# A Swin layer with a dynamic convolution behind it: where the convolution's pieces and its taps stand in the order of the work

## The chip, the cores and the metric

The kernel runs on one core of a Trainium2 chip. The metric is the device time of one execution in microseconds. Before the change it was 3257.63 us, the median of 3 runs (3256.80 to 3258.41).

## What is computed

The input is x, 16 images of 192 channels and 56 x 56 pixels, in float32. Two layers follow one another:

```python
# layer 0: one Swin block, windows of 7 x 7, shifted by 3, 6 heads of 32
h = layernorm(x over channels); h = roll(h, -3, -3); cut into 64 windows of 49 tokens
q, k, v = h @ qkv_w + qkv_b
attn = softmax(q * 32**-0.5 @ k.T + rel_bias + mask) @ v
x1 = x + roll_back(attn @ proj_w + proj_b)
y = gelu(layernorm(x1) @ fc1_w + fc1_b) @ fc2_w + fc2_b      # 192 -> 768 -> 192
x = x1 + y
# layer 1: a depthwise 3 x 3 convolution whose taps depend on the image
pooled = x.mean over pixels
t = relu(gamma * (pooled @ w1.T - running_mean) / sqrt(running_var + eps) + beta)
taps = (t @ w2.T + b2) * causal_mask          # 4 of the 9 taps are not zero
out = depthwise_conv(x, taps) + bias
```

The taps of an image need the mean over all its pixels, so its convolution can start only when the image has left layer 0.

## The kernel before

**Steps.** An image is held in SBUF as two tiles: x0 for channels 0 to 127 and x1 for the other 64, upper half of the rows in partitions 0 to 63 and lower half in 64 to 127. Each has one more row 0 in front, which the convolution reads as the row above. A step `i` is one row of windows in each half of an image (16 windows, handled as eight by two); an image has STEPS = 4 steps, the whole input NS = 64. The main loop (L975) is a pipeline: its turn `i` does the MLP of step i-2 (mlp_first, mlp_wide, mlp_narrow), the attention of step i, q, k and v of step i+1, the layer-norm statistics of steps i+2 and i-1, and pieces of the convolution of the last finished image.

**Order.** The schedule is written out by hand (`tc.manual_schedule`): each engine runs its instructions in the order in which the program issues them; semaphores between engines are put in from the tiles. PSUM is four pairs of banks, `pair0` to `pair3`, taken by name through `banks(name, k)`; the four letters A, B_, C, D of a turn say which is which, and the turn ends with `pairs = [C, B_, D, A]`. So the next turn's first ph tile takes this turn's C, its second B_, its third D, its fourth A.

**One turn on TensorE**: ph (first MLP layer: three long and three short products, then f = 3 to 5 short; st, the statistics, in pair C; f = 3 to 5 long), sc (scores, first of them in pair C again), pq, pe, pk (q and k), pf (second MLP layer, wide half) with the transposes pt between, po (attention times v), pf (narrow half), pp (projection) and pv (v of the next step).

**What the change touches.**
- `attention_v_out` (L437) copies v from PSUM (two tiles pv, in pairs D and A; each has two banks, index h) to the block-diagonal operand `vbd` (L204): 16 copies, of which VectorE has those with j = 0 (L450) and ScalarE those with j = 1 (L452), two and two by turns.
- `norm1_scale` (L310) is twelve products into the window tiles (L328, L336), in the main loop on VectorE.
- `conv_begin` (L679) starts a piece of 14 rows on ScalarE (`y = tap1 * x + bias`, L683); `conv_rest` (L692) adds three taps on VectorE (L698), for pieces 3 and 5 with a copy of the bias into one row (L707), and issues the output DMAs on SP (L716, L718). An image has six pieces; `conv_ready(k)` hands out up to k.
- In a turn the first piece is in `between` (L986): behind three gelus and the three short products, ahead of the statistics and of `norm_vars` (L280 on ScalarE, L282 on VectorE). The second has its `conv_begin` at L1041, behind the gelu table load, and its `conv_rest` at L1050, between mlp_narrow and the narrow `mlp_out` (L641).
- `residual` (L571) adds the projection to x1 (L578, from pp1) and to x0 (L582, from pp).
- `taps_pool` and `taps` (L646 to L677) run once per image, in the turn in which its last step leaves the MLP: a sum (L648), three copies into the rows 0 (L650 on GpSimd, L651 and L652 on VectorE), four matmuls into a tile t of pair C, and five VectorE operations (L661 to L676) that end with the taps `wt`. They are issued behind v's matmuls and ahead of `attention_v_out` (L1064).
- `norm_squares` (L238) for the second norm: squares on ScalarE (L243, L244), a sum on GpSimd (L250).

Of the kernel before, what the change touches and what calls it, by code (L numbers as in the profile page):

```python
# [36 lines left out]
def tile_swin_then_dynamic_conv(  # L37
# [163 lines left out]


    kbd = one.tile([128, 3, NWIN, 2, N], F32, tag="kbd", name="kbd")
    vbd = const.tile([128, 2, NWIN, HEADS // 2, 64], F32, tag="vbd", name="vbd")  # L204
    prob = [
        const.tile([128, 2 * HEADS, 64], F32, tag=f"prob{i}", name=f"prob{i}") for i in range(4)
    ]
# [229 lines left out]
    def attention_v_out(pvs):  # L437

        for blk, pv in enumerate(pvs):
            src = pv.rearrange("p h (w n) -> p h w n", w=2)[:, :, :, 0:DIM]  # L440
            src = src.rearrange("p h w (g j d) -> p h w g j d", j=2, d=HD)
            for s in range(2):
                for j in range(2):
                    for h in range(2):
                        dst = vbd[j * 64 : j * 64 + N, h].rearrange(
                            "p (b w s) g (j d) -> p b w s g j d", b=2, s=2, j=2
                        )[:, blk, :, s, :, j, :]
                        f = src[s * 64 : s * 64 + N, h, :, :, j, :]
                        if j == 0:
                            nc.vector.tensor_copy(dst, f)  # L450
                        else:
                            nc.scalar.copy(dst, f)  # L452

    def attention_scores(i, q4, q2, ks):

# [62 lines left out]
    def attention_weigh(po, po1, wp, prt):  # L518
        for s in range(2):
            w = wp * 2 + s  # L520
            for a, g in ((0, 0), (0, 1), (1, 0), (1, 1), (0, 2), (1, 2)):

                r, k = (g, a) if g < 2 else (a, 2)
                o = po[:, a] if g < 2 else po1
                at = (g if g < 2 else a) * 64
                mm(
                    o[at : at + 64, w * N : (w + 1) * N],
                    vbd[:, a, w, g, :],
                    prt[:, r, k * PW + s * 64 : k * PW + s * 64 + N],
                    True,  # L530
                    True,
                )
# [17 lines left out]

    def project(i, o, k, k1):

        pp, pp1 = banks(f"pp_{i}", k), banks(f"pp1_{i}", k1)[:, 0]

        def narrow():
            for a in range(2):
                mm(pp1[a * 64 : a * 64 + 64, :T], wp0[:, C0:DIM], o[:, a], True, False)

        def rest():
            for a in range(2):  # L560
                p = slice(a * 64, a * 64 + 64)
                mm(pp[:, a, :T], wp1[p], o[p, 2], True, False)

        def whole():
            mm(pp1[:, :T], wp2, o[:, 2], False, True)
            for a in range(2):
                mm(pp[:, a, :T], wp0[:, 0:C0], o[:, a], False, True)

        return pp, pp1, narrow, rest, whole

    def residual(i, pp, pp1):  # L571
        v0, v1 = rows_of(i)
        q1 = pp1[:, :T].rearrange("p (r c) -> p r c", c=IMG)
        q0 = pp[:, :, :T].rearrange("p h (r c) -> p h r c", c=IMG)
        rolls = ((0, IMG - SHIFT, SHIFT), (IMG - SHIFT, IMG, 0))
        for lo, hi, to in rolls:
            xs = v1[:, :, to : to + hi - lo]
            nc.vector.scalar_tensor_tensor(xs, q1[:, :, lo:hi], pb[1], xs, ALU.add, ALU.add)  # L578
        for a in range(2):
            for lo, hi, to in rolls:  # L580
                xs = v0[:, a, :, to : to + hi - lo]
                nc.vector.scalar_tensor_tensor(xs, q0[:, a, :, lo:hi], pb[0], xs, ALU.add, ALU.add)  # L582

    def mlp_first(i, yn, hid, ks, between):
# [12 lines left out]

        for f in range(3):
            take(f)
            long(dsts[f], wf1, cols(f), y0, True)  # L600
        for f in range(3):
            short(dsts[f], wf1, cols(f), y1, False)
            gelu(f)
        for f in range(3, NFC):
            take(f)
            short(dsts[f], wf1, cols(f), y1, True)
        between()
        for f in range(3, NFC):
            long(dsts[f], wf1, cols(f), y0, False)
            gelu(f)  # L610
# [35 lines left out]
    def taps_pool(b):  # L646
        pooled = small.tile([128, 2, 1], F32, tag="pooled", name=f"pooled_{b}")
        nc.vector.tensor_reduce(pooled, sums.pop(b), AX.X, ALU.add)  # L648
        x0, x1 = images[b]
        nc.gpsimd.tensor_copy(x0[:, 0, :], x0[:, IMG, :])  # L650
        nc.vector.tensor_copy(x1[0:64, 0, :], x1[64:128, HALF, :])  # L651
        nc.vector.tensor_copy(x1[64:128, 0, :], x1[0:64, HALF, :])  # L652
        return pooled

    def taps(b, pooled, k):

        pt = banks(f"t_{b}", k)[:, 0]
        for kc in range(2):
            mm(pt[:, 0:RED], pooled[:, kc].broadcast_to([128, 128]), w1t[:, kc], kc == 0, kc == 1)
        tt = small.tile([128, 1, RED], F32, tag="tt", name=f"tt_{b}", bufs=1)  # L660
        nc.vector.tensor_tensor(tt[:, 0], pt[:, 0:RED], bn[:, 0], ALU.mult)  # L661
        nc.vector.tensor_tensor(tt[:, 0], tt[:, 0], bn[:, 1], ALU.add)
        tw = small.tile([128, 2 * NTAP, RED], F32, tag="tw", name=f"tw_{b}", bufs=1)
        nc.vector.scalar_tensor_tensor(
            tw,
            tt.broadcast_to([128, 2 * NTAP, RED]),
            0.0,
            w2n.rearrange("p k t r -> p (k t) r"),
            ALU.max,
            ALU.mult,  # L670
        )
        wt = small.tile([128, 2, NTAP], F32, tag="wt", name=f"wt_{b}")
        nc.vector.tensor_reduce(
            wt.rearrange("p k (t o) -> p (k t) o", o=1), tw, AX.X, ALU.add
        )
        nc.vector.tensor_tensor(wt, wt, b2t, ALU.add)  # L676
        return wt  # L677
# [72 lines left out]
    def tail_of(i, o, kp, kv):  # L750

        pvs, v_rest, v_whole = attention_v(i + 1, kv) if has(i + 1) else (None, None, None)
        if o is not None:
            pp, pp1, narrow, rest, whole = project(i, o, kp, 3)
# [83 lines left out]
    for t in [kbd, vbd] + prob:  # L838
        nc.gpsimd.memset(t, 0.0)
    keys = stats_of(-1)  # L840
    dev = norm_devs(keys)
# [66 lines left out]
    def taps_weights():  # L908
# [66 lines left out]
    for i in range(2, NS + 2):  # L975
        A, B_, C, D = pairs
        keys = {}


        if has(i + 1):  # L980
            norm1_scale(i + 1, dvs.pop(0), nc.vector)
        if (i + 3) % STEPS == 0 and (i + 3) // STEPS < B:
            b = (i + 3) // STEPS
            images[b] = load_x(b, nc.sync)

        def between():  # L986
# [9 lines left out]
        mlp_first(i - 2, yns.pop(i - 2), hid, (A, B_, C, D, A, B_), between)  # L996
        for part, dev in var:
            table(AF.Sqrt)
            norm_root(part)
# [46 lines left out]
        if has(i):  # L1046
            o = attention_rows(i, attention_values(i, prts, D, C))
        pf1 = mlp_narrow(i - 2, hid, A)
        for c in ys:
            conv_rest(*c)  # L1050
        mlp_out(i - 2, 1, pf1[:, :T])
        if has(i):
            pp, pp1, p_narrow, p_rest, p_whole = project(i, o, B_, C)
            p_narrow()
            p_rest()
        if has(i + 1):
# [1 line left out]
            v_rest()  # L1058
        if has(i):
            p_whole()  # L1060
            residual(i, pp, pp1)
# [87 lines left out]
```

## Time and profile before

| | |
|---|---|
| median of 3 runs | 3257.63 us |
| the profiled execution, its own time | 3261.49 us |
| its span, first to last instruction | 3259.7 us |
| granted TensorE clock, mean | 0.981 |
| busy: PE / DVE / ACT / POOL | 3128.8 / 2155.5 / 1855.1 / 1020.4 us |
| y taps L698 (VectorE), x288 | 321.0 us, mean 1116 ns |
| v's copies L450 (VectorE), x512 | 159.2 us, mean 349 ns |
| v's copies L452 (ScalarE), x512 | 135.4 us, mean 312 ns |

PE is TensorE's matmuls, PEld its weight loads, DVE is VectorE, ACT is ScalarE, POOL is GpSimd, SP issues the DMAs. A matmul in float32 stands as two instructions. In a timeline line the columns are: start and length in us, engine, line, operation, out<-in, shapes, how many; in brackets the idle time of the engine just before and what ended it. In the list of waits they are: who waited for whom, us in total, how often, the longest.

### The profile page before, as it was taken

Reading aid. Unit: us, or ns where it says so; the run is one execution under the profiler, and the core shown is the slowest. Engines: PE = TensorE matmul, PEld = TensorE weight load, DVE = VectorE, ACT = ScalarE, POOL = GpSimd, SP = SyncE. Lnnn points to the kernel's source line nnn. Section 1 sums busy time; section 2 is a strip of 40 time slices with the busy share of each in tenths; the row PEclk is TensorE's granted clock in tenths of the full one; section 3 lists DMA queues with packets and bytes.
Section 4 is the critical chain, followed back from the end, with each engine's and each line's share of the span. In section 5 each row is a group of like instructions: output and inputs, shape, how many; then the busy total and the mean of one; then the engine's idle time right before and its main releaser. Section 6 shows DMA issues by size and latency. Waiting matters only on the chain.

```text
span 3259.7 us, 64143 instructions
## 1 busy us (share of the span) xinstructions
PE 3128.8 (96%) x26130; PEld 1938.8 (59%) x26130; DVE 2155.5 (66%) x3893; ACT 1855.1 (57%) x2988; POOL 1020.4 (31%) x912
## 2 busy tenths in 40 slices
PE   5699999999999999999999999999999999999996
PEld 3456566666666656666666656666665666666653
DVE  4345666766767676676776766676676767667664
ACT  2445655655655665565665565565565565566552
POOL 4333233233233223333323323323323323323220
PEclk7699999999999999999999999999999999999998
DMA  3001012121111202102111111202111120201101
GB/s 99 12 19 48 20 40 56 31 60 31 33 53 36 61 26 65 31 26 60 37 51 36 54 29 39 55 30 62 31 32 55 36 59 28 65 25 31 26 31 45
DMA packets 79123, 135.35 MB, mean 42 GB/s; under 512 B 21766, under 2 KB 61692, under 8 KB 76908
## 3 DMA queue, kind: packets, MB, share of 16 engines
q1 hardware_dynamic: 77266, 128.54, 14.0%
q8 instruction: 206, 3.38, 0.4%
q0 software_dynamic: 1056, 1.92, 0.3%
q10 hardware_dynamic: 506, 0.79, 0.1%
q14 instruction: 89, 0.73, 0.1%
HBM read 41.25 MB, written 38.54 MB: 24 GB/s over the span
## 4 chain that ended last, share of the span: by engine, by line
PE 89%; DVE 4%; ACT 2%; issue 1%; POOL 0%; DMA 0%; ACTq 0%; DVEq 0%; POOLq 0%
PE ph L92 23%; PE pf L92 22%; PE pv L92 7%; PE pp L92 7%; PE po L92 5%; PE pq L92 4%; PE pt L509 4%; PE sc L92 4%; PE st L92 4%; PE pe L92 4%; PE pk L92 4%; DVE y L698 1%; DVE vbd L450 1%; DVE y L707 1%; ACT vbd L452 1%
## 5 line engine op out<-in xcount | busy, mean ns | idle before, releaser
L92 PE MATMUL ph<-yn,wf 128*128 128x392 f32 (+1 forms) x3072 | 811.4, 501 | 27.3 <-ACT vbd L452 18.8
L92 PE MATMUL pf<-hid,wf 128*128 128x392 f32 (+1 forms) x3072 | 802.8, 494 | 3.5 <-ACT hid L596 2.0
L496 POOL TENSOR_TENSOR prob<-e,tot 113x588 f32<-113x588 f32 x256 | 298.1, 1176 | 1165.8 <-DVE tot L495 1151.3
L92 PEld LDWEIGHTS ph<-yn,wf 128*128 128x128 f32 (+1 forms) x3072 | 425.4, 189 | 384.4 <-issue 91.6
L452 ACT COPY vbd<-pv 49x192 f32<-49x192 f32 x512 | 135.4, 312 | 768.1 <-DVE vbd L450 767.8
L92 PEld LDWEIGHTS pf<-hid,wf 128*128 128x128 f32 (+1 forms) x3072 | 386.4, 164 | 303.6 <-issue 119.9
L698 DVE SCALAR_TENSOR_TENSOR y<-x,wt,y 128x770 f32<-128x770 f32 x288 | 321.0, 1116 | 214.8 <-ACT y L683 208.1
L596 ACT ACTIVATE hid<-ph,f1b 128x784 f32<-128x784 f32 x384 | 336.8, 912 | 127.7 <-PE ph L92 127.3
L250 POOL TENSOR_TENSOR sq<-sq,sq 64x392 f32<-64x392 f32 x256 | 262.9, 1027 | 383.1 <-ACT sq L244 368.6
L347 POOL TENSOR_TENSOR yn<-x,dv 128x784 f32<-128x784 f32 x64 | 129.2, 2019 | 574.6 <-DMA dv<-dev 541.8
L92 PEld LDWEIGHTS pv<-wqkv,win 64*128 64x128 f32 (+1 forms) x2048 | 259.4, 190 | 47.5 <-DVE x L641 7.7
L92 PE MATMUL pv<-wqkv,win 64*128 64x192 f32 (+1 forms) x2048 | 277.1, 328 | 7.7 <-DVE x L641 4.4
L480 DVE TENSOR_TENSOR e<-sc,bias_t 113x588 f32<-113x588 f32 x256 | 179.6, 763 | 149.5 <-PE sc L92 149.4
L487 DVE TENSOR_TENSOR e<-e,top 113x588 f32<-113x588 f32 x256 | 265.7, 1038 | 8.9
L641 DVE SCALAR_TENSOR_TENSOR x<-pf,cols,x 128x784 f32<-128x784 f32 (+1 forms) x128 | 105.8, 827 | 232.8 <-PE pf L92 225.7
L92 PE MATMUL pp<-o,wp 128*128 128x392 f32 (+2 forms) x896 | 253.0, 517 | 2.6 <-ACT o L545 2.6
L235 ACT ACT_TABLE_LOAD x192 | 246.3, 1283 | 3.4
L515 ACT COPY prt<-pt 128x678 f32<-128x678 f32 x256 | 179.1, 726 | 118.1 <-PE pt L509 116.5
L490 ACT ACTIVATE e<-e 113x588 f32<-113x588 f32 x256 | 176.7, 691 | 107.6 <-DVE e L487 105.2
L450 DVE COPY vbd<-pv 49x192 f32<-49x192 f32 x512 | 159.2, 349 | 97.0 <-ACT vbd L452 82.9
L509 PEld LDWEIGHTS pt<-ident,prob 113*128 113x128 f32 x1536 | 167.3, 142 | 76.1 <-issue 47.0
L92 PE MATMUL po<-prt,vbd 128*64 128x49 f32 x6144 | 199.9, 225 | 0.2 <-ACT prt L515 0.2
(143 smaller groups left out, 4073.3 us busy)
## 6 DMA issues: line engine op xcount, KB each, us to landing
dv<-dev SPq DMA_DIRECT2D x1020, 49.0 KB
x<-in_x_dram SPq DMA_DIRECT2D x15, 1484.0 KB
out_dram<-y SPq DMA_DIRECT2D x48, 392.0 KB
out_dram<-y SPq DMA_DIRECT2D x48, 196.0 KB
x<-in_x_dram SPq DMA_DIRECT2D x16, 392.0 KB
x<-in_x_dram SPq DMA_DIRECT2D x15, 350.0 KB
out_dram<-y SPq DMA_DIRECT2D x16, 308.0 KB
out_dram<-y SPq DMA_DIRECT2D x16, 154.0 KB
```

Of the source, the lines that this page charges most:

```text
L92: nc.tensor.matmul(dst, lhs, rhs, start=start, stop=stop, skip_group_check=True)
L235: nc.scalar.activation(junk, eps_t[0:1], func)
L250: nc.gpsimd.tensor_tensor(s0[p, h], s0[p, h], s1[p], ALU.add)
L450: nc.vector.tensor_copy(dst, f)
L480: nc.vector.tensor_tensor(e, sc[:PW, :, : HEADS * N], rel, ALU.add)
L487: nc.vector.tensor_tensor(ehs[wp], ehs[wp], t.broadcast_to([PW, 2 * HEADS, N]), ALU.subtract)
L490: nc.scalar.activation(es[wp], es[wp], AF.Exp)
L496: nc.gpsimd.tensor_tensor(prob[wp][:PW, :, 0:N], ehs[wp], t.broadcast_to([PW, 2 * HEADS, N]), ALU.mult)
L509: nc.tensor.transpose(pt[:, a, g * PW : (g + 1) * PW], prob[wp][:PW, h : h + 2, :].rearrange("p h k -> p (h k)"), ident[:PW, :PW],)
L515: nc.scalar.copy(prt, pt[:, :, : 3 * PW])
L596: nc.scalar.activation(hid[:, f], phs[f][:, :, :T], AF.Gelu, bias=f1b[:, f : f + 1])
L698: nc.vector.scalar_tensor_tensor(dst, src, wt[:, kc, t : t + 1], dst, ALU.mult, ALU.add)
```

## The change

1. Conv: `conv_ready(2)` at the head of the turn. The first piece's `conv_begin` is issued at once, ahead of norm1_scale and of all gelus; a new `after()`, called in `mlp_first` behind the first three gelus, issues the second piece's `conv_begin` and then both `conv_rest`. The places in `between` and around `mlp_narrow` are gone.
2. v: `vbd` becomes two tiles, one per h. VectorE makes all copies of h = 0, ScalarE all of h = 1.
3. Taps: the sum and the four t matmuls are issued behind the projection's last matmuls, ahead of the residual and of v's long matmuls; t lies in the second bank of the pair whose first bank is pp1. In the residual, between its x1 and x0 parts, one add makes tt (`taps_hidden`). The copies into the rows 0, all three now on VectorE (`taps_rows`), and the rest of the network (`taps_out`) are issued behind `attention_v_out` and `norm_squares`. The multiplication of t by the batch norm's scale is gone; w1t is scaled once at the start instead, by two products.

```diff
-    vbd = const.tile([128, 2, NWIN, HEADS // 2, 64], F32, tag="vbd", name="vbd")
+    vbd = [
+        const.tile([128, NWIN, HEADS // 2, 64], F32, tag=f"vbd{h}", name=f"vbd{h}")
+        for h in range(2)
+    ]
...
-            for s in range(2):
-                for j in range(2):
-                    for h in range(2):
...
-                        if j == 0:
-                            nc.vector.tensor_copy(dst, f)
-                        else:
-                            nc.scalar.copy(dst, f)
+            for h, copy in enumerate((nc.vector.tensor_copy, nc.scalar.copy)):
+                for s in range(2):
+                    for j in range(2):
...
+                        copy(dst, src[s * 64 : s * 64 + N, h, :, :, j, :])
...
-    def residual(i, pp, pp1):
+    def residual(i, pp, pair1, between=None):
...
             nc.vector.scalar_tensor_tensor(xs, q1[:, :, lo:hi], pb[1], xs, ALU.add, ALU.add)
+        if between:
+            between()
         for a in range(2):
...
             short(dsts[f], wf1, cols(f), y1, False)
             gelu(f)
+        after()
...
+    def taps_rows(b):
+
         x0, x1 = images[b]
-        nc.gpsimd.tensor_copy(x0[:, 0, :], x0[:, IMG, :])
+        nc.vector.tensor_copy(x0[:, 0, :], x0[:, IMG, :])
         nc.vector.tensor_copy(x1[0:64, 0, :], x1[64:128, HALF, :])
         nc.vector.tensor_copy(x1[64:128, 0, :], x1[0:64, HALF, :])
...
+    def taps_hidden(b, pt):
         tt = small.tile([128, 1, RED], F32, tag="tt", name=f"tt_{b}", bufs=1)
-        nc.vector.tensor_tensor(tt[:, 0], pt[:, 0:RED], bn[:, 0], ALU.mult)
-        nc.vector.tensor_tensor(tt[:, 0], tt[:, 0], bn[:, 1], ALU.add)
+        nc.vector.tensor_tensor(tt[:, 0], pt[:, 0:RED], bn[:, 1], ALU.add)
+        return tt
...
+        for k in range(2):
+            nc.vector.tensor_tensor(w1t[:, k], w1t[:, k], s, ALU.mult)
...
+        cs = conv_ready(2)
+        ys = [conv_begin(*c) for c in cs[:1]]
         if has(i + 1):
             norm1_scale(i + 1, dvs.pop(0), nc.vector)
+
+        def after():
+            ys.extend(conv_begin(*c) for c in cs[1:])
+            for c, y in zip(cs, ys):
+                conv_rest(*c, y)
...
         def between():
-            for b, wt, n in conv_ready(1):
-                conv_rest(b, wt, n, conv_begin(b, wt, n))
...
-        ys = [(*c, conv_begin(*c)) for c in conv_ready(1)]
...
-        for c in ys:
-            conv_rest(*c)
...
             p_whole()
-            residual(i, pp, pp1)
+        b, pt, at = (i - 2) // STEPS, None, lambda: None
+        if (i - 2) % STEPS == STEPS - 1:
+            pt = taps(b, taps_pool(b), pair1[:, 1] if has(i) else banks(f"t_{b}", C)[:, 0])
+            convs.append({"b": b, "n": 0})
+
+            def at():
+                convs[-1]["tt"] = taps_hidden(b, pt)
+
+        if has(i):
+            residual(i, pp, pair1, at)
+        else:
+            at()
         if has(i + 1):
             v_whole()
-        if (i - 2) % STEPS == STEPS - 1:
-            b = (i - 2) // STEPS
-            convs.append({"b": b, "n": 0, "wt": taps(b, taps_pool(b), C)})
-        if has(i + 1):
             attention_v_out(pvs)
         if has(i):
             norm_squares(f"2_{i}", i, 1, nc.scalar)
+        if pt is not None:
+            taps_rows(b)
+            convs[-1]["wt"] = taps_out(b, convs[-1]["tt"])
```

More of the change, by code (lines that the diff above doesn't have):

```diff
@@ L441, in attention_v_out @@
             src = src.rearrange("p h w (g j d) -> p h w g j d", j=2, d=HD)
-            for s in range(2):
-                for j in range(2):
-                    for h in range(2):
-                        dst = vbd[j * 64 : j * 64 + N, h].rearrange(
+            for h, copy in enumerate((nc.vector.tensor_copy, nc.scalar.copy)):
+                for s in range(2):
+                    for j in range(2):
+                        dst = vbd[h][j * 64 : j * 64 + N].rearrange(
                             "p (b w s) g (j d) -> p b w s g j d", b=2, s=2, j=2
                         )[:, blk, :, s, :, j, :]
-                        f = src[s * 64 : s * 64 + N, h, :, :, j, :]
-                        if j == 0:
-                            nc.vector.tensor_copy(dst, f)
-                        else:
-                            nc.scalar.copy(dst, f)
+                        copy(dst, src[s * 64 : s * 64 + N, h, :, :, j, :])
     def attention_scores(i, q4, q2, ks):
@@ L527, in attention_weigh @@
                     o[at : at + 64, w * N : (w + 1) * N],
-                    vbd[:, a, w, g, :],
+                    vbd[a][:, w, g, :],
                     prt[:, r, k * PW + s * 64 : k * PW + s * 64 + N],
@@ L551, in project @@
     def project(i, o, k, k1):
-        pp, pp1 = banks(f"pp_{i}", k), banks(f"pp1_{i}", k1)[:, 0]
+        pp, pair1 = banks(f"pp_{i}", k), banks(f"pp1_{i}", k1)
+        pp1 = pair1[:, 0]
         def narrow():
@@ L567, in whole @@
                 mm(pp[:, a, :T], wp0[:, 0:C0], o[:, a], False, True)
-        return pp, pp1, narrow, rest, whole
-    def residual(i, pp, pp1):
+        return pp, pair1, narrow, rest, whole
+    def residual(i, pp, pair1, between=None):
         v0, v1 = rows_of(i)
-        q1 = pp1[:, :T].rearrange("p (r c) -> p r c", c=IMG)
+        q1 = pair1[:, 0, :T].rearrange("p (r c) -> p r c", c=IMG)
         q0 = pp[:, :, :T].rearrange("p h (r c) -> p h r c", c=IMG)
@@ L582, in residual, with mlp_first @@
                 nc.vector.scalar_tensor_tensor(xs, q0[:, a, :, lo:hi], pb[0], xs, ALU.add, ALU.add)
-    def mlp_first(i, yn, hid, ks, between):
+    def mlp_first(i, yn, hid, ks, after, between):
         y0, y1 = [yn[0][:, h] for h in range(2)], yn[1]
@@ L648, in taps_pool, with taps, taps_out @@
         nc.vector.tensor_reduce(pooled, sums.pop(b), AX.X, ALU.add)
+        return pooled
+    def taps_rows(b):
         x0, x1 = images[b]
-        nc.gpsimd.tensor_copy(x0[:, 0, :], x0[:, IMG, :])
+        nc.vector.tensor_copy(x0[:, 0, :], x0[:, IMG, :])
         nc.vector.tensor_copy(x1[0:64, 0, :], x1[64:128, HALF, :])
         nc.vector.tensor_copy(x1[64:128, 0, :], x1[0:64, HALF, :])
-        return pooled
-    def taps(b, pooled, k):
-        pt = banks(f"t_{b}", k)[:, 0]
+    def taps(b, pooled, pt):
         for kc in range(2):
             mm(pt[:, 0:RED], pooled[:, kc].broadcast_to([128, 128]), w1t[:, kc], kc == 0, kc == 1)
+        return pt
+    def taps_hidden(b, pt):
         tt = small.tile([128, 1, RED], F32, tag="tt", name=f"tt_{b}", bufs=1)
-        nc.vector.tensor_tensor(tt[:, 0], pt[:, 0:RED], bn[:, 0], ALU.mult)
-        nc.vector.tensor_tensor(tt[:, 0], tt[:, 0], bn[:, 1], ALU.add)
+        nc.vector.tensor_tensor(tt[:, 0], pt[:, 0:RED], bn[:, 1], ALU.add)
+        return tt
+    def taps_out(b, tt):
         tw = small.tile([128, 2 * NTAP, RED], F32, tag="tw", name=f"tw_{b}", bufs=1)
@@ L753, in tail_of @@
         if o is not None:
-            pp, pp1, narrow, rest, whole = project(i, o, kp, 3)
+            pp, pair1, narrow, rest, whole = project(i, o, kp, 3)
             narrow()
@@ L760, in tail_of @@
             whole()
-            residual(i, pp, pp1)
+            residual(i, pp, pair1)
         if pvs:
@@ L837, in tile_swin_then_dynamic_conv @@
     nc.vector.tensor_scalar(kb, pick, qkb[:, 1:2], None, ALU.mult)
-    for t in [kbd, vbd] + prob:
+    for t in [kbd] + vbd + prob:
         nc.gpsimd.memset(t, 0.0)
@@ L995, in tile_swin_then_dynamic_conv @@
         hid = one.tile([128, NFC, 2, T], F32, tag="hid", name=f"hid_{i - 2}")
-        mlp_first(i - 2, yns.pop(i - 2), hid, (A, B_, C, D, A, B_), between)
+        mlp_first(i - 2, yns.pop(i - 2), hid, (A, B_, C, D, A, B_), after, between)
         for part, dev in var:
@@ L1048, in tile_swin_then_dynamic_conv @@
         pf1 = mlp_narrow(i - 2, hid, A)
-        for c in ys:
-            conv_rest(*c)
         mlp_out(i - 2, 1, pf1[:, :T])
         if has(i):
-            pp, pp1, p_narrow, p_rest, p_whole = project(i, o, B_, C)
+            pp, pair1, p_narrow, p_rest, p_whole = project(i, o, B_, C)
             p_narrow()
@@ L1060, in tile_swin_then_dynamic_conv @@
             p_whole()
-            residual(i, pp, pp1)
+        b, pt, at = (i - 2) // STEPS, None, lambda: None
[8 more added lines that the diff above has]
+            at()
         if has(i + 1):
             v_whole()
-        if (i - 2) % STEPS == STEPS - 1:
-            b = (i - 2) // STEPS
-            convs.append({"b": b, "n": 0, "wt": taps(b, taps_pool(b), C)})
-        if has(i + 1):
             attention_v_out(pvs)
```

## The prediction

> **What bounds the kernel now.** I read the page first (busy shares, the chain that ended last), then who waited for whom on TensorE, then the timeline around one step of each kind.
>
> ```profile
> span 3259.7 us, 64143 instructions
> ...
> PE 3128.8 (96%) x26130; PEld 1938.8 (59%) x26130; DVE 2155.5 (66%) x3893; ACT 1855.1 (57%) x2988; POOL 1020.4 (31%) x912
> ...
> PE 89%; DVE 4%; ACT 2%; issue 1%; POOL 0%; DMA 0%; ACTq 0%; DVEq 0%; POOLq 0%
> ```
>
> TensorE is the bound: 96% busy and 89% of the chain. Only what makes PE wait is worth time. PE's own waits (engine, line, whom; then us in total, times, longest):
>
> ```profile
> PE ph L92 <- ACT vbd L452: 18.8, 16, 3.3
> ...
> PE ph L92 <- DVE tt L661: 5.9, 15, 0.4
> PE pv L92 <- DVE x L641: 4.4, 11, 0.5
> ```
>
> The first two come 15 times in the loop, once per image, and name the lines that the change moves. The timeline of one such place (start, us, engine, line):
>
> ```profile
> 1531.73 0.18 DVE L652 COPY x<-x 64x56 f32<-64x56 f32 x1
> 1531.78 0.54 PE L92 MATMUL t<-w1t,pooled 128*128 128x48 f32 x4
> 1532.36 0.21 DVE L661 TENSOR_TENSOR tt<-t,bn 128x48 f32<-128x48 f32 x1 [0.45 <-PE t L92]
> ...
> 1532.71 2.87 PE L92 MATMUL ph<-yn,wf 128*128 128x392 f32 x8 [0.39 <-DVE tt L661]
> ...
> 1534.11 0.17 DVE L676 TENSOR_TENSOR wt<-wt,b2t 128x8 f32<-128x8 f32 x1
> 1534.20 0.61 DVE L450 COPY vbd<-pv 49x192 f32<-49x192 f32 x2
> 1534.89 0.53 ACT L452 COPY vbd<-pv 49x192 f32<-49x192 f32 x2 [13.24 <-DVE vbd L450]
> ...
> 1536.70 1.58 PE L92 MATMUL ph<-yn,wf 128*128 128x392 f32 x4 [1.11 <-ACT vbd L452]
> ```
>
> At an image's end VectorE does the whole taps network (L661 to L676) before v's copies (L450); the third ph tile wants v's PSUM pair back and stands 1.11 us. In numbers, from first ph matmul to first ph matmul: an undisturbed step takes 47.67 us (1776.61 to 1824.28), the taps step 48.61 (1678.79 to 1727.39), the step after it 49.21 (1727.39 to 1776.61). Excess: 0.94 + 1.54 = **2.48 us per image**, 15 images inside the loop. The pv wait lengthens eleven or so conv steps by 0.6 to 0.77 us (1582.01 to 1630.42 is 48.41); over all steps I count 7.5 us.
>
> VectorE's stretch before the scores, in an undisturbed conv step:
>
> ```profile
> 1582.01 8.26 PE L92 MATMUL ph<-yn,wf 128*128 128x392 f32 x36
> ...
> 1586.69 2.17 POOL L250 TENSOR_TENSOR sq<-sq,sq 64x392 f32<-64x392 f32 x2 [4.64 <-ACT sq L244]
> 1586.77 1.20 DVE L336 TENSOR_TENSOR win<-x,dv 64x28 f32<-64x28 f32 x2
> ...
> 1590.54 3.13 DVE L698 SCALAR_TENSOR_TENSOR y<-x,wt,y 128x770 f32<-128x770 f32 x3 [1.27 <-ACT y L683]
> ...
> 1593.70 1.14 DVE L282 TENSOR_TENSOR dev<-st,dev 64x392 f32<-64x392 f32 x2
> ```
>
> PE's first score matmul comes at 1596.46. I count in each step from O, its first ph matmul (here 1582.01): scores at O+14.45. They take the PSUM pair that L282 reads, so L282 has to be done by then; it ends at O+12.83. This is the slack that the change spends.
>
> **What the skill says.** The Trainium skill, SBUF — State Buffer, section "Who interferes with whom": VectorE and GpSimd share one port pair, an exclusive lock; its section on the two sides adds that a VectorE instruction with two SBUF inputs takes part. The trace agrees: two L336 of 64x28 take 1.20 us beside POOL's L250, two of 64x21 after it 0.36 (at 1588.91). Same skill, PSUM — Partial Sum Buffer, "PSUM bank collisions raise a hardware error": two engines may not be in one bank and quadrant at once, reads included. That fits the alternation of L450 and L452 in the trace (each idles 0.65 to 0.70 us between its pairs), since both read both banks of pv. Perfetto Trace Analysis, "Identifying the Most-Contended Engine": busy time of matmuls measures headroom badly; so I use step lengths.
>
> **The change part by part.** The sum is for the profiled execution, 3261.49 us (span 3259.7); the median of the three runs is 3257.63, so I carry the difference over.
>
> 1. *Taps' network beside the projection.* The four t matmuls go between pp and pv; PE still pays them, 0.4 us (1531.95 to 1532.34 in the chain). Their wait for L661 (0.39) and the wait for v's copies (the rest of 2.48) go: v's copies now come right behind the residual. Excess per image falls from 2.48 to 0.4: 15 x 2.08 = **-31.2**. One multiply (L661) goes into w1t.
>
> 2. *v's operand as two tiles, one bank per engine.* VectorE does bank 0, ScalarE bank 1, no hand-over. VectorE's eight copies take 7 starts of 0.275 plus 0.34, some 2.2 us instead of 3.8 (1580.93 to 1584.74). In an undisturbed step pv's second half ends at O+0.16, so they end at O+1.35 instead of O+2.73. No PE time in itself (ph's third tile is reached at O+2.65), but it pays for part 3. If the hand-over stayed, 1.4 us of this would be lost in each step.
>
> 3. *Both conv pieces in the first layer.* Removed from the second layer: the piece ahead of mlp_out's narrow half (L641), so the pv wait goes: **-7.5**. SP's output DMAs of that piece now come before the dv transfers, not behind them. Added: a second piece ahead of L282, three L698, 3.13 us.
>  Second and third conv step of an image: copies end O+1.35; norm1_scale 4.6 (1584.66 to 1589.27, with the lock's share, 3.2 without); two pieces 6.3; a bias copy 0.2; L282 1.15: **O+13.6**, slack 0.8. ScalarE: copies and squares end near O+2.6, the y piece ahead of the gelus 1.05, first gelu due at O+5.05: hidden. The second y piece stands behind the gelus, where the old one stood.
>  Step after taps: pair1 holds t beside pp1. The trace's L582 waits for the last matmul of the whole pp pair, though its first half was done 0.66 us earlier; so I let L578 wait for t as well, which ends at O-2.44. L578 0.75, tt 0.21, L582 1.41: O-0.1. Copies 2.2: O+2.1. Three row copies (one came from POOL), 0.19 each: O+2.65. L664, L673, L676: 1.35, O+4.0. norm1_scale with the lock 4.6: O+8.6. Two pieces 6.25: O+14.85. L282 1.15: **O+16.0**. Late by 1.55. Behind L282 in PE's order stand the scores and everything after them: 15 x 1.55 = **+23.3**. The y piece ahead of the gelus waits there for wt (O+4.0 to 5.3) and may hold st a few tenths; that overlaps the same wait.
>  Bounds of this term: if L578 doesn't wait for t (0.65 less) and the lock costs nothing (1.4 less), no wait at all; another blocked POOL operation of 1.05 makes it 2.6. So 0 to 39 us; I take 23.3.
>
> 4. *Once.* Start: ph after the second prologue step waits to 177.67 for the alternating copies, pv ends at 174.35; -2.1. Two more small multiplies on w1t ahead of L282 at 154.78: +0.45; earlier scores at 127: -0.2. Together -1.9 (0 to -4). End: POOL's yn at 3202.01 starts as L698 ends, 1.1 later than its transfer allows: -1.1; in the last taps the row copies leave the shadow of t, +0.57, L661 goes, -0.2. Together **-0.7**.
>
> Sum: -31.2 + 23.3 - 7.5 - 1.9 - 0.7 = **-18.0**. 3261.5 becomes 3243.5; the median 3257.6 becomes 3239.6, say **3240**.
>
> **The rivals.**
> *The new wait hardly comes* (below 0.9 us per image): t's bank is told from pp1's, or POOL's squares fall beside PSUM copies, which show no lock. For it: L450 runs 0.34 us beside L250. At 0.3 us: -41.3 + 4.5 = -36.8, 3221. Chance 0.22.
> *The wait eats nearly all* (2.2 to 3.0 us): POOL's two L250 block taps_out and then the windows as well. About -3, 3254. Chance 0.13.
> *Slower: VectorE overfull in every conv step.* Place: the stretch from the copies to L282. L698 has two SBUF inputs; beside POOL's yn one takes 1.70 instead of 1.02. If the moved passes pay one more round of the lock, 1.44, in each conv step, the late two are 0.64 over and the first 2.99: 30 x 0.64 + 15 x 2.99 = 64.1, against -41.3 (all other terms): +22.8, 3280. It decides from 0.93 us more per step: 15 x (1.55 + 0.93) + 30 x (0.93 - 0.8) = 41. Against it: POOL has only its two L250 there, idle for the rest until O+22. Chance 0.10. That the split does nothing, the hand-over staying for another reason, ends in the same place and is counted here.
>
> **How the numbers follow.** Forecast (wait 0.9 to 2.2, 3230 to 3249): 0.55; hardly any wait 0.22; nearly all eaten 0.13; slower 0.10. The range reaches from no wait at all, 3218, to a wait of 2.6, 3256. A measurement of this kernel tells about 0.2%, 6.5 us, from no change. Faster by more: 0.55 + 0.22 + a quarter of 0.13 = 0.80; within: 0.09; slower: 0.11.
>
> **What would show it.** Taps steps at 48.1 us, late conv steps at 47.7, no PE wait for vbd, tt or L641. In the step after taps, PE's sc waiting 1 to 2 us for DVE's L282, and that step near 49.2, where the 1.54 of before had another name. L578 starting after t. The forecast is wrong if sc waits in the second and third conv steps too (slower), or if it waits nowhere (faster than said).

## The result, and the profile after

| | before | after |
|---|---|---|
| median of 4 runs each, side by side | 3257.22 us (3253.80 to 3258.41) | 3253.31 us (3252.57 to 3258.02) |
| ratio of the times | | 0.9993, 95% interval 0.9975 to 1.001 |
| the profiled execution: own time, span | 3261.49, 3259.7 us | 3253.62, 3251.8 us |
| turns 3 to 62 in the profile | 2904.7 us | 2900.6 us |

No change that can be told from none; 3240 was forecast. The three lines of the page of after that answer to those of before:

```profile
span 3251.8 us, 64181 instructions
...
PE 3123.3 (96%) x26130; PEld 1937.1 (60%) x26130; DVE 2115.2 (65%) x3895; ACT 1887.8 (58%) x2988; POOL 991.6 (30%) x897
...
PE 85%; DVE 9%; issue 2%; POOL 1%; ACT 0%; DMA 0%; SPq 0%; DVEq 0%; POOLq 0%; ACTq 0%
```

TensorE is as busy as before, and VectorE is less busy by 40 us in all (2155.5 to 2115.2). Still VectorE's part of the chain has grown from 4% to 9%. Less work on an engine, and more of it in the way: so look for one place. TensorE's waits in after:

```profile
PE sc L92 <- DVE dev L285: 23.1, 15, 1.5
...
PE ph L92 <- ACT hid L598: 3.5, 15, 0.2
PE ph L92 <- ACT vbd L451: 3.2, 1, 3.2
```

The waits for tt and for the x of mlp_out are gone, and the wait for v's copies is gone but for one at the start. In their place stands one that was not there: the scores, 15 times 1.5 us, for L285 (L282 of before). By kind of turn, from first ph matmul to first ph matmul (means of 15 each):

| turn | before | after | change x 15 |
|---|---|---|---|
| taps | 48.61 | 48.12 | -7.3 us |
| after taps | 49.18 | 49.89 | +10.6 us |
| second and third conv turn | 47.85, 48.00 | 47.68, 47.68 | -7.4 us |

One kind of turn gives back 10.6 of the 14.7 us that the other three bring. The timeline of such a turn in after (its first ph matmul, O, is at 1721.69):

```profile
1718.64 0.54 PE L92 MATMUL pp<-w1t,pooled 128*128 128x48 f32 x4
...
1719.22 0.75 DVE L578 SCALAR_TENSOR_TENSOR x<-pp,cols,x 128x371 f32<-128x371 f32 x2 [4.46 <-PE pp L92]
...
1720.00 1.40 DVE L584 SCALAR_TENSOR_TENSOR x<-pp,cols,x 128x371 f32<-128x371 f32 x4
1721.32 2.94 DVE L451 COPY vbd<-pv 49x192 f32<-49x192 f32 x8
...
1722.86 1.29 ACT L451 COPY vbd<-pv 49x192 f32<-49x192 f32 x4 [11.75 <-DVE vbd L451]
...
1724.35 1.29 ACT L451 COPY vbd<-pv 49x192 f32<-49x192 f32 x4 [0.20 <-DVE vbd L451]
...
1727.02 2.32 POOL L253 TENSOR_TENSOR sq<-sq,sq 64x392 f32<-64x392 f32 x2 [6.14 <-ACT sq L247]
1727.13 2.59 DVE L339 TENSOR_TENSOR win<-x,dv 64x343 f32<-64x343 f32 x2
...
1728.86 1.74 PE L92 MATMUL ph<-yn,wf 64*128 64x392 f32 x8 [0.23 <-ACT hid L598]
...
1730.90 6.18 DVE L708 SCALAR_TENSOR_TENSOR y<-x,wt,y 128x770 f32<-128x770 f32 x6
...
1737.11 1.14 DVE L285 TENSOR_TENSOR dev<-st,dev 64x392 f32<-64x392 f32 x2
...
1738.40 1.32 PE L92 MATMUL sc<-kbd,q 64*64 64x98 f32 x52 [1.54 <-DVE dev L285]
```

From L578 on, no gap of VectorE is longer than 0.04 us: everything in this stretch adds up, and its end, 1738.25 or O+16.56, sets the scores, O+16.71, which stand at O+14.45 in a turn without a wait. So they are 2.26 us late, though the profile shows only 1.54 of it as a wait for L285. The forecast had O+16.0 for that end. Two readings inside the stretch: eight copies take 2.94 us, not 2.2; and ScalarE's two groups of four copies start 0.09 us after VectorE's four of the same pv tile (at 1722.77 and 1724.26), although the two engines read different banks.

### The profile page after: what moved, and what is told of

It is laid out like the page before. It is cut to its first block, busy times and chain, and to the rows that moved or that the text cites. A ratio compares the mean times of both kernels' runs of the same rounds, so it can differ in the third digit from the quotient of the medians.

```text
span 3251.8 us, 64181 instructions
## 1 busy us (share of the span) xinstructions
PE 3123.3 (96%) x26130; PEld 1937.1 (60%) x26130; DVE 2115.2 (65%) x3895; ACT 1887.8 (58%) x2988; POOL 991.6 (30%) x897
## 4 chain that ended last, share of the span: by engine, by line
PE 85%; DVE 9%; issue 2%; POOL 1%; ACT 0%; DMA 0%; SPq 0%; DVEq 0%; POOLq 0%; ACTq 0%
PE pf L92 23%; PE ph L92 19%; PE pp L92 7%; PE pv L92 6%; PE po L92 6%; PE pt L508 4%; PE pq L92 4%; PE sc L92 4%; PE pk L92 4%; PE pe L92 4%; PE st L92 3%; DVE y L708 3%; DVE win L339 1%; DVE vbd L451 1%; DVE x L584 1%
## 5 line engine op out<-in xcount | busy, mean ns | idle before, releaser
L451 ACT COPY vbd<-pv 49x192 f32<-49x192 f32 x512 | 160.6, 314 | 704.2 <-DVE vbd L451 699.5
L253 POOL TENSOR_TENSOR sq<-sq,sq 64x392 f32<-64x392 f32 x256 | 263.7, 1030 | 369.5 <-ACT sq L247 354.9
L708 DVE SCALAR_TENSOR_TENSOR y<-x,wt,y 128x770 f32<-128x770 f32 x288 | 314.0, 1104 | 16.6 <-ACT y L693 8.4
L350 POOL TENSOR_TENSOR yn<-x,dv 128x784 f32<-128x784 f32 x64 | 119.0, 1859 | 571.3 <-DMA dv<-dev 549.1
L92 PEld LDWEIGHTS po<-prt,vbd 128*64 128x64 f32 x6144 | 191.9, 140 | 9.4 <-ACT prt L514 0.6
```

The source lines that it names most:

```text
L92: nc.tensor.matmul(dst, lhs, rhs, start=start, stop=stop, skip_group_check=True)
L253: nc.gpsimd.tensor_tensor(s0[p, h], s0[p, h], s1[p], ALU.add)
L451: copy(dst, src[s * 64 : s * 64 + N, h, :, :, j, :])
L708: nc.vector.scalar_tensor_tensor(dst, src, wt[:, kc, t : t + 1], dst, ALU.mult, ALU.add)
```

## The experiments

Theory at the outset: the mechanism of the prediction holds, the gain of its parts 1 and 2 and of the removed wait for mlp_out's x was made, and the second conv piece in the turn after taps costs all of it, because VectorE's stretch there is longer than summed. Rivals: the gain of the taps' part never came, or VectorE is overfull in every conv turn.

The part ahead of the loop can't be compared between single profiles. In before and conv_alone, which are alike there, the loop starts at 177.67 and 171.44 us; over all kernels it starts between 167 and 178. So I compare the turns 3 to 62 (TensorE's first ph of turn 3 to that of turn 63) and the kinds of turn, which repeat within 0.02 us inside a profile, but for single turns and for conv turns that wait for mlp_out's x (47.7 to 48.5 us in before). A turn is what the prediction calls a step; turn 34 is the one in the table's last column. Line numbers shift by a line or two between the kernels: L451 of after is L452 in v_by_halves, L285 is L282 in before.

| kernel | time, us (runs) | ratio, 95% interval | turns 3 to 62, us | turn after taps, us |
|---|---|---|---|---|
| before | | | 2904.7 | 49.21 |
| after | 3253.3 (4) | 0.9993, 0.9975 to 1.001 | 2900.6 | 49.94 |
| e1_conv_back | 3224.9 (4) | 0.9905, 0.9888 to 0.9921 | 2871.4 | 47.68 |
| e2_conv_alone | 3282.2 (1) | | 2931.5 | 50.47 |
| e3_pieces_1221 | 3228.5 (4) | 0.9913, 0.9898 to 0.9927 | 2877.8 | 48.32 |
| e4_no_sums | 3229.4 (1) | | 2877.0 | 48.37 |
| e5_v_by_halves | 3235.3 (1) | | 2891.1 | 49.31 |
| e6_x1_first | 3244.5 (1) | | 2890.7 | 49.28 |
| e7_v_alone | 3256.8 (1) | | 2904.3 | 49.42 |
| e8_1221_y_behind | 3218.2 (4) | 0.9894, 0.9872 to 0.9915 | 2866.8 | 47.68 |
| e9_halves_alternating | 3247.4 (1) | | 2897.9 | 49.73 |
| e10_1221_y_behind_halves | 3213.0 (4) | 0.9869, 0.9852 to 0.9885 | 2866.6 | 47.68 |

Each ratio is against runs of before beside it, which had medians of 3255.67 (e1 to e4), 3254.32 (e5 to e8) and 3256.10 us (e9, e10).

### e1_conv_back: taps and v as changed, the conv pieces where they stood

```diff
-        cs = conv_ready(2)
-        ys = [conv_begin(*c) for c in cs[:1]]
...
         def after():
-            ys.extend(conv_begin(*c) for c in cs[1:])
-            for c, y in zip(cs, ys):
-                conv_rest(*c, y)
+            pass
...
         def between():
+            for b, wt, n in conv_ready(1):
+                conv_rest(b, wt, n, conv_begin(b, wt, n))
...
+        ys = [(*c, conv_begin(*c)) for c in conv_ready(1)]
...
         pf1 = mlp_narrow(i - 2, hid, A)
+        for c in ys:
+            conv_rest(*c)
```

> Taps and v as changed, the convolution's two pieces back where they stood. My theory (VectorE's stretch ahead of L285 in the step after taps is too long by the second piece): that step falls from 49.94 to 47.7 us, no wait of sc, and the pv wait behind the late piece comes back, 0.6 to 0.8 in some steps, 7.5 in all; span 3251.8 - 33.9 + 7.5 = 3225. Rival (ScalarE's late copies and the y piece ahead of the gelus hold TensorE, VectorE doesn't): only the 0.23 us of ph's wait goes, 3.5 in all; span about 3256.

Measured: 3224.9 us, 0.9905. The turn after taps has no wait. The wait that the conv part removes is back, in seven turns:

```profile
PE pv L92 <- DVE x L644: 2.8, 7, 0.5
```

The taps' part and v's split are worth 33 us of the loop's 2904.7, so the rival in which the taps' gain never came falls; so does the one above, ScalarE alone, for which 3.5 us were to go. Taking the conv pieces into the first layer then costs 29 (2871.4 to 2900.6): 33.9 in the turns after taps, with 4.6 won in the late conv turns.

Why the second piece is dear in one turn and nearly free in the others is seen in VectorE's idle time. A third conv turn of this run (O at 1804.19):

```profile
1812.73 3.13 DVE L708 SCALAR_TENSOR_TENSOR y<-x,wt,y 128x770 f32<-128x770 f32 x3 [2.85 <-ACT y L693]
1815.90 1.14 DVE L285 TENSOR_TENSOR dev<-st,dev 64x392 f32<-64x392 f32 x2
```

VectorE stands idle for 2.85 us until ScalarE has made the y piece. In after, the two pieces begin in that time, and L285 ends at O+14.11 instead of O+12.85. In the turn after taps there is no such idle time: L285 ends at O+13.54 here and at O+16.56 in after, later by a whole piece.

### e2_conv_alone: before, with the conv part only

The edit is the conv part of the diff shown above, on the kernel before: `conv_ready(2)`, `after()`, and the old places gone.

> The kernel before with only the convolution's pieces moved. My theory: the step after taps, whose L282 ended 14.98 us after its first ph matmul, ends 3.1 later; scores at 18.25 instead of 15.99, the step 51.5 us instead of 49.2; pv waits go; span 3259.7 + 33.9 - 7.5 = 3286, slower than both. Rival (the moved piece is free in itself, it is the taps' new place that costs): span about 3252.

Measured: 3282.2 us, the loop 26.8 us longer than before; the rival falls. That 26.8 is near the expected 33.9 - 7.5 = 26.4 is luck. The turns after taps give 18.6 and not 33.9: turn 34 takes 50.47 us and not 51.5, as L282 ends 2.2 us later and not 3.1, since VectorE had stood idle for 0.86 us ahead of its piece there. And the late conv turns, which were to gain 7.5, lose 8.1: the second and third conv turn wait as well (48.23 us, scores at O+15.01), 43 waits in all:

```profile
PE sc L92 <- DVE dev L282: 17.4, 43, 0.5
```

VectorE's copies show why. In a third conv turn (O at 1833.51) they take from 1832.43 to 1836.23, with 0.65 us of idle time between the groups:

```profile
1832.43 0.61 DVE L450 COPY vbd<-pv 49x192 f32<-49x192 f32 x2
...
1833.68 1.28 DVE L450 COPY vbd<-pv 49x192 f32<-49x192 f32 x4 [0.65 <-ACT vbd L452]
...
1835.60 0.63 DVE L450 COPY vbd<-pv 49x192 f32<-49x192 f32 x2 [0.65 <-ACT vbd L452]
```

So "VectorE overfull in every conv turn" is what happens without v's split, which takes 0.55 us off each of the late conv turns. With the split this rival falls for after: there L285 ends at O+14.11 in a late conv turn, 0.34 ahead of need.

### e3_pieces_1221: the conv's six pieces spread over four turns

```diff
-        cs = conv_ready(2)
+        cs = conv_ready((2, 1, 1, 2)[i % STEPS])
...
+        if i % STEPS == 1:
+            for c, y in zip(cs, ys):
+                conv_rest(*c, y)
+            cs = []
```

The turn after taps has one piece, the next two have two each, and the following taps turn has the last.

> As changed, but the six pieces spread as 1, 2, 2, 1 over the four steps of the next image instead of 2, 2, 2, 0; the last one is issued ahead of the load into its image's buffers. My theory: VectorE's stretch behind taps is 3.1 us shorter, sc waits nowhere, each image costs three steps of 47.68 and one of 48.12; span 3251.8 - 15 x 2.26 = 3218, time about 3220. Rival (ScalarE ahead of the gelus): the y piece still stands there, the step after taps gains little; span about 3250.

Measured: 3228.5 us, 0.9913: the wait of the scores goes, but not all that was expected came. The turn after taps still takes 48.32 us, not 47.68. What is left there:

```profile
1712.98 1.03 ACT L693 ACTIVATE y<-x,cols,wt 128x784 f32<-128x784 f32 x1
...
1714.03 2.52 ACT L598 ACTIVATE hid<-ph,f1b 128x784 f32<-128x784 f32 x3
...
1714.99 1.73 PE L92 MATMUL ph<-yn,wf 64*128 64x392 f32 x8 [0.23 <-ACT hid L598]
```

ScalarE's first gelu comes at O+6.21 (O at 1707.82), behind its late copies, the squares and the y piece. The bracket shows 0.23 us of waiting; the turn is 0.64 longer. The profile models where matmuls end, which may hide the rest; the length of the turn is the surer reading. That ScalarE is the cause is tested in e8.

### e4_no_sums: GpSimd's two additions behind taps left out

```diff
-        for h in range(2):
+        for h in range(2 if add else 0):
             p = slice(h * 64, h * 64 + 64)
             nc.gpsimd.tensor_tensor(s0[p, h], s0[p, h], s1[p], ALU.add)
...
-            norm_squares(f"2_{i}", i, 1, nc.scalar)
+            norm_squares(f"2_{i}", i, 1, nc.scalar, pt is None)
```

This leaves part of the second norm's sum of squares out of the computation, once per image.

> As changed, but behind an image's taps GpSimd's two additions of squares are left out, so that step's second norm lacks the squares of 64 channels. My theory: without the lock L339 takes 0.52 instead of 1.3 twice, VectorE is 1.5 us earlier at L285; scores at 15.2 instead of 16.71, the step 48.4; span 3251.8 - 22.6 = 3229. Rival (the lock falls into time that VectorE has anyway): no difference, 3252.

Measured: the turn after taps 48.37, time 3229.4 us. The two products L339 of 64x343 take 1.03 us where they took 2.59 beside POOL's L253:

```profile
1715.59 1.03 DVE L339 TENSOR_TENSOR win<-x,dv 64x343 f32<-64x343 f32 x2
...
1724.02 1.14 DVE L285 TENSOR_TENSOR dev<-st,dev 64x392 f32<-64x392 f32 x2
```

L285 ends 1.56 us earlier, at O+15.00 (O at 1710.16). This is the exclusive lock between VectorE and GpSimd that the prediction took from the Trainium skill, SBUF — State Buffer, "Who interferes with whom". The trace agrees: both additions beside two-input products cost VectorE 1.56 us, where the prediction had 1.4. Still this turn is 0.69 us longer than 47.68, as that of e3 is, with the same 0.22 us of ph waiting for the first gelu.

### e7_v_alone: before, with v's split only

The edit is the v part of the diff above, on the kernel before.

> The kernel before with v's two tiles alone. My theory (no copies side by side within one pv tile): behind taps VectorE's four copies of the first pv tile end at +1.47, ScalarE's four only after them at +2.85, 0.4 later than the last of before; the third ph tile waits longer, that step 49.6 instead of 49.2, others unchanged; span 3259.7 + 6 = 3266. Rival (one bank per engine lets them run side by side): the tile is free 0.9 earlier, the step 48.3, span 3246.

Measured: the turn after taps is longer, 49.42 against 49.21, where the rival had it shorter; half of the 0.4 that the theory expected. The loop is the same within 0.4 us, since the waits for mlp_out's x became fewer. Nothing of the split shows as time by itself, and the profile has the hand-over:

```profile
1724.42 2.95 DVE L451 COPY vbd<-pv 49x192 f32<-49x192 f32 x8
1725.96 1.28 ACT L451 COPY vbd<-pv 49x192 f32<-49x192 f32 x4 [14.00 <-DVE vbd L451]
1727.30 0.96 PEld L92 LDWEIGHTS ph<-yn,wf 128*128 128x128 f32 x4 [2.03 <-ACT vbd L451]
```

ScalarE idles through VectorE's first four copies, and TensorE waits for ScalarE. Its single time, 3256.8, lies among those of before beside it (3247.1 to 3259.2), so it tells nothing.

### e5_v_by_halves and e9_halves_alternating: what the copies cost

In e5 the two tiles of v's operand stand for the halves of the windows, so each engine has one whole pv tile; each group of two copies has its partitions in common:

```diff
-            for h, copy in enumerate((nc.vector.tensor_copy, nc.scalar.copy)):
-                for s in range(2):
-                    for j in range(2):
+            copy = (nc.vector.tensor_copy, nc.scalar.copy)[blk]
+            for s in range(2):
+                for j in range(2):
+                    for h in range(2):
```

> As changed, but v's two operand tiles hold the windows' two halves: VectorE copies all of the first pv tile, ScalarE all of the second, two copies after each other on the same partitions. My theory (copies that change partitions start only when the one before has ended, 0.37 instead of 0.275 each; and the two engines may not read one pv tile at once, whatever its banks): VectorE 2.55 instead of 2.94 us for its eight, ScalarE's eight end 1.3 earlier and ph's wait for hid goes; scores at 16.3 instead of 16.71, span 3245.6. Rival (the hand-over is no matter of pv's tile): ScalarE's copies still stand behind VectorE's, no gain, 3252 or above.

e9 is e5 with another order of the same copies, so that the output's partitions change with every one:

```diff
             for s in range(2):
-                for j in range(2):
-                    for h in range(2):
+                for h in range(2):
+                    for j in range(2):
```

> Tells apart the two parts of what v_by_halves gained in the step after taps (49.94 to 49.31 us): copies that start in pairs on the same partitions, and two engines that no longer share a tile. Here each engine still has a tile of its own, but the order of the copies is such that input or output partitions change with every copy. Theory (a copy starts only after the end of the one before it when the partitions change): VectorE's eight copies take 2.9 us instead of 2.55, ScalarE's eight 2.6 instead of 2.2 and start with their own tile, so no wait of ph for a gelu; L285 ends 0.4 later than with pairs, scores at O+16.5, the step after taps 49.7, span about 3239. Rival (only the shared tile cost time): copies as with pairs, the step 49.3, span 3233.

Measured: the turn after taps 49.31 (e5) and 49.73 (e9), after 49.94. The time of e5, 3235.3, lies below what was expected, mostly because its loop starts at 167.44 us, where that of after, from which it was reckoned, starts at 174.88. That of e9 lies above, mostly because it was reckoned from e5, and its own loop starts at 172.48. In the loop e5 gains 9.5 us on after, and e9 2.7. The copies, e5 and then e9:

```profile
1709.44 2.53 DVE L452 COPY vbd<-pv 49x192 f32<-49x192 f32 x8
...
1710.01 2.15 ACT L452 COPY vbd<-pv 49x192 f32<-49x192 f32 x8 [10.78 <-PE pv L92]
...
1714.61 1.04 ACT L694 ACTIVATE y<-x,cols,wt 128x784 f32<-128x784 f32 x1 [1.15 <-DVE wt L687]
```

```profile
1717.44 2.92 DVE L452 COPY vbd<-pv 49x192 f32<-49x192 f32 x8
...
1718.01 2.58 ACT L452 COPY vbd<-pv 49x192 f32<-49x192 f32 x8 [10.78 <-PE pv L92]
```

So the two parts come apart. Order: 0.4 us on either engine, for the same eight copies, and 0.42 us of the turn. Two copies on the same partitions start 0.27 us apart on VectorE, two on other partitions 0.37, each only when the one before has ended.

The Trainium skill says so for VectorE, VectorE: DVE Perf Modes, "Two Vector instructions with no wait between them": a held instruction "starts only when every earlier Vector instruction has finished", and it is held when its start quadrant isn't that of the one before; the traces agree. In the change's order (window half s, column half j) the output's half changes with every copy, so none starts early. With one bank per engine the four copies of a pv tile all differ in the half they read or write, so by that page no order of the loops over s and j mends it.

A tile of one's own: ScalarE starts its copies as pv's matmuls end and not behind VectorE; with it the turn is 0.21 us shorter (after against e9). What both show besides is that freeing ScalarE doesn't free its gelus: it now idles 1.15 us ahead of the y piece, for wt. In e5 the wait of ph for the gelus is gone; in e9, where it was expected to go too, 15 waits remain, 2.7 us in all.

### e6_x1_first: the residual's x1 part ahead of t

```diff
             p_whole()
+            residual(i, pp, pair1, None, (1,))
...
-            residual(i, pp, pair1, at)
+            residual(i, pp, pair1, at, (0,))
```

> As changed, but the residual's x1 part (L578) is issued ahead of the t matmuls. My theory (L578 waits for t only since t lies in the tile of pp1 and is issued earlier): L578 starts 1.3 us earlier, beside pp, and all of VectorE's stretch ends 0.55 earlier; scores at 16.16 instead of 16.71, span 3251.8 - 8.2 = 3243.6. Rival (t's own wait decides, L578 is only in its shadow): no difference, 3252.

Measured: the turn after taps 49.28, 0.66 less than in after; 3244.5 us. This is the cost of t's lying in the pair of pp1, which L578 reads: the prediction had 0.65 for it. As in after, TensorE waits 1.53 us for L285; it only reaches the scores sooner, as ph no longer waits for the gelus (first gelu at O+5.54).

### e8_1221_y_behind and e10_1221_y_behind_halves: a better order

e8 is e3 with the y piece behind the gelus in the turn after taps:

```diff
-        ys = [conv_begin(*c) for c in cs[:1]]
+        ys = [] if i % STEPS == 2 else [conv_begin(*c) for c in cs[:1]]
...
-            ys.extend(conv_begin(*c) for c in cs[1:])
+            ys.extend(conv_begin(*c) for c in cs[len(ys) :])
```

> The spread 1, 2, 2, 1, and behind taps the y piece is issued after the three gelus instead of ahead of them. My theory (the 0.65 us left in that step with the spread is ScalarE's: late copies, squares and the y piece push the first gelu from 5.05 to 6.2): the step falls from 48.32 to 47.68, no wait of ph for hid; span 3223.0 - 15 x 0.65 = 3213, time about 3215. Rival (those 0.65 are VectorE's): 3223 again.

Measured: 3218.2 us, 0.9894. No wait is left in the loop; the turn after taps takes 47.68:

```profile
1708.96 2.53 ACT L598 ACTIVATE hid<-ph,f1b 128x784 f32<-128x784 f32 x3
...
1716.06 1.14 DVE L285 TENSOR_TENSOR dev<-st,dev 64x392 f32<-64x392 f32 x2
...
1718.13 2.24 PE L92 MATMUL sc<-kbd,q 64*64 64x98 f32 x96
```

The first gelu starts at O+5.28 (O at 1703.68), L285 ends at O+13.52 and the scores start at O+14.45 without a bracket. That is the 0.64 us of e3, gone with its cause.

e10 is e8 with e5's halves.

> The version with pieces 1, 2, 2, 1 and the y piece behind the gelus in the step after taps (3218.2 us), with v's operand by halves of the windows as well. Theory: nothing waits in the loop of that version, so faster copies gain nothing there: all steps 47.68, taps steps 48.12, and 3218 within 3 us. Rival (what v_by_halves gained outside the step after taps, some 7 us at the start, is real and not chance): 3210 to 3212, with the loop starting at 167 instead of 171.

Measured: 3213.0 us, 0.9869. In the profile the loop is that of e8 (2866.6 against 2866.8 us), so faster copies gain nothing there, and it starts at 172.10. But the profiled execution is the slowest of the four, 3218.7; the others took 3210.4 to 3214.6, near what the rival said, and no profile shows where their loops started. Whether the 7 us at e5's start were chance stays open. That e10 is faster than e8 is not shown: the intervals of the ratios overlap. Both are faster than before and than after.

## Why the prediction was wrong, by its own steps

**What bounds, and where to look: right.** Only TensorE's waits moved the time, and the new one stands where it was forecast, for the instruction that was forecast, 15 times. That the profile shows it as 1.54 us, and 1.55 was forecast, is luck: TensorE also comes late to the scores, for the gelus (e3, 0.64), and the delay is 2.26.

**1. Taps' network: right.** Its excess in the taps turn was to be 0.4 and is 0.45. The waits for tt and v's copies went; e1 shows the turn after taps at 47.68. The forecast -31.2 is 15 x (0.49 + 1.55) = -30.6 in e1's kinds of turn.

**2. v's two tiles: wrong.** "No hand-over", "7 starts of 0.275 plus 0.34, some 2.2 us": the hand-over between the engines stayed, by pv tile, and VectorE's copies take 2.94. The prediction put the alternation of before down to both engines' reading both banks; with one bank each ScalarE still follows VectorE (e7). And I took the 0.275 from before, where two copies in a row had the same partitions, and didn't ask whether the new order keeps that. The case "if the hand-over stayed" was named, but with the loss on VectorE; it fell on ScalarE. In a turn without taps its copies and squares end at O+4.55, where O+2.6 was counted, and in the turn after taps the copies alone end at O+3.95.

**3. The second piece in the first layer: the mechanism right, the size wrong. This is the step that failed: the delay of the scores in the turn after taps, sized at 1.55 us per image, is 2.26.** The part's -7.5 came: the second and third conv turns give -7.4. The late conv turns have no wait, though the same copies leave 0.34 of the slack of 0.8. For the turn after taps it said "Copies 2.2: O+2.1" and "O+16.0. Late by 1.55". Step by step, with the lines above: L578 waits for t, as assumed (e6: 0.66); the residual ends at O-0.29 (said: O-0.1); the copies end at O+2.57 (said: O+2.1); row copies and taps_out end at O+4.57 (said: O+4.0); norm1_scale with the lock takes 4.6 (said: 4.6; e4 shows the lock's 1.56); two pieces 6.2 (said: 6.25); L285 ends at O+16.56, 0.56 later than said. The copies, 2.94 long, begin 0.08 before the residual ends, so they add 0.66 more than was counted; the row copies and taps_out add 0.1 more, and the residual is 0.19 early. On top, the scores start 0.15 after L285 has ended. The term left that out, though the trace of before showed it: ph starts at 1532.71, and L661, which it waited for, ends at 1532.57. So 0.56 + 0.15 = 0.71 us per image, 2.26 instead of 1.55: the term is +33.9, not +23.3.

With that one term the sum -18.0 becomes -7.4, and the span fell by 7.9; that the two are so near is in part chance. In the loop, -4.8 would follow and -4.1 were measured.

**4. Once: open.** Outside the turns 3 to 62 the span fell by 3.8, where -2.6 was forecast, but single profiles scatter there by more than that.

**ScalarE's "few tenths": right in after, and a trap behind it.** The y piece comes late behind the copies and squares, not for wt as was said. The late gelus cost 0.65 us per image, but inside VectorE's wait. Only when e3 and e4 took that wait away did they show.

**The rivals.** The time landed at "nearly all eaten" (3254), with a wait of 2.26 inside its 2.2 to 3.0. Its cause was another: it had GpSimd blocking taps_out as well, while taps_out was over before the additions began, and the lock cost what the forecast had counted. "Slower" with late conv turns that wait describes e2, the conv part without v's split. That e2 took 3282 and this rival had 3280 is chance: the 3280 holds the gain of the taps' part, which e2 lacks. The hand-over that stayed was counted with this rival, and it did not make the kernel slower. The lower end of the range, 3218 for no wait at all, is 3216 by the prediction's own terms.

**The reckoning of the change.** Without the conv part it saves 33 us of the loop; the conv part then gives 29 back, though it adds no work: three L708, 3.1 us, are moved ahead of L285. In the late conv turns they fall into time in which VectorE was idle; in the turn after taps there is none, L285 had only 0.9 us left before the scores (e1: O+13.54 against O+14.45), and GpSimd's additions fall into the same stretch. Spread by what each turn has room for, and with the y piece behind the gelus in the turn after taps, the same pieces bring no wait (e8).

## What to carry to other kernels

Before work is moved into a stage, sum that stage's chain on its engine for each kind of turn by itself, its idle time too, and let the sum say which turn takes the work: moved work is cheap where the engine stood idle, and costs its whole length where it didn't. A time from start to start, read where two copies in a row have the same partitions, holds only for that order (here 0.27 us); where each copy changes partitions, count the whole copy (here 0.37). And where two engines finish late for the same turn, taking one away shows the other, so look at both before counting a gain.

## What the runs showed that the prediction had not expected

- Eight copies of 49x192 out of PSUM take 2.53 us on VectorE in pairs on the same partitions and 2.92 alternating; on ScalarE 2.15 and 2.58. The prediction had one interval for every copy.
- Two engines that read different banks of one tile still follow one another: ScalarE's copies start 0.09 us after VectorE's end. This is the program's wait, for with a tile each (e9) the same copies overlap.
- GpSimd's two additions of 64x392 cost VectorE about as much in two places where they meet other instructions: in after two L339 of 64x343 take 2.59 instead of 1.03 us; in e9 an addition of 128x8 (L687) takes 0.81 instead of 0.17, and the two L331 behind it 1.75 instead of 0.95.
